# Two-layer metaformer with a mixture of experts: the taps of the second image's convolution moved from TensorE to VectorE, and its scatters paced

## The chip, the cores and the metric

The kernel runs on one core of one Trainium2 chip. The metric is the device time of one execution in microseconds; the lower the better. A core has TensorE (PE, matrix products; PEld is its weight load), VectorE (DVE), ScalarE (ACT), GpSimd (POOL) and SyncE (SP), which only issues transfers. Each has its own queue of instructions, and they meet through semaphores. Times of the kernel before are the median of three runs; the profile is of one execution of its own.

## The reference

The input is four images of 384 channels and 32 × 32 pixels, all in float32. Two layers follow, each a mixer and then a feed-forward part, with a residual sum around each:

```
x = x + attention(LN_c(x))           # layer 0, 8 heads, relative positions
t = t + kron_ffn(LN_t(t))
x = x + conv(LN_c(x))                # layer 1: 7x7 + 5x3 + 3x5 + 7x1*1x7 + 5x1*1x5, per channel
t = t + moe(LN_t(t))                 # 4 experts, best 2 of each token
```

The five convolutions of layer 1 act on each channel alone, so their sum is one 7 × 7 convolution with 49 taps per channel (folded beforehand in the kernel). The mixture of experts sends each of 4 × 1024 tokens to the two experts with the highest gate (384 → 1536 → 384 with a gelu between) and adds the two results, weighted by the gates.

## The kernel before

Channels lie on the 128 partitions in three chunks (`k`), tokens along the free axis. The attention runs first (to about 1540 us of the profiled execution) and the change doesn't touch it. Everything below is in `rest_phase`.

**Per image.** `front` (project L977, net L999 to L1030) loads an image and its attention result, projects, runs the first feed-forward network in two halves of 512 tokens, and `normalise` (L1051) prepares the layer norm of the convolution. `image` (L1065) writes the normalised image into the padded tile `img`, of which there is one. `convolve` (L1079) runs the 49 taps on VectorE: one `scalar_tensor_tensor` (L1089) per tap and part, where a part is some rows of one chunk; 32 rows are 1024 columns. `taps_by_matmul` (L1125) does taps on TensorE instead, with diagonal 64 × 64 weights, two taps to a pair (`tap_ps`, L1137), a sum over both halves (`taps_ps`, L1148) and an addition by VectorE (L1151). The diagonals lie in the second expert weight buffer `wts[1]`, so this buffer is not free for experts until the last such matmul. `gates` (L1184) computes the gate logits (`gate_ps`, L661) and picks two experts per token; `scatter` (L1223) works out each token's place and writes its rows out by 16 indirect transfers that GpSimd issues one by one (`write`, L1205). `dispatch` is `gates` and `scatter` together. These are Python generators: each `yield` is a step, and most give a pair of estimated costs (VectorE, TensorE) in us.

**Experts.** The scattered rows form 67 blocks of 128 rows, in four groups of 13, 16, 16 and 22 (`COUNTS`). Group g can begin when image g's scatters are done: its first gathers (`xg`, L1250) wait for all of them. A block is 12 steps of 6 + 2 matmuls (`e_ps` L1301, `y_ps` L1279), with gelu on ScalarE between (L1304) and the output's bias on VectorE (`yo`, L1282). Weights come in halves by indirect transfers on GpSimd's queue (L1269), three ahead; where the expert stays the same as two blocks before, the transfer moves nothing.

**Order.** The tile framework orders instructions per engine by program order unless an instruction is free to move up; `pin` and `keep_in_program_order` hold an instruction where it was written. In `convolve` the taps of image 0 alone are pinned. In the later images a tiny `pause` memset per step (L1097) is kept in order. `first` runs image 0's convolution with TensorE's taps and image 1's front between its steps. Then `dispatch(0)` is issued with image 1's TensorE taps and image 2's front dealt among its steps. The rest is one long generator, `todo = others()`: the convolution of images 1 to 3 with the front of the next image and the dispatch of the one before between the taps. The blocks call `more` 12 times each; it adds 0.05 to `clock[0]` (VectorE's account) and 1.36 to `clock[1]` (TensorE's) and takes steps from `todo` while the first is below the second, each step adding its costs. So the costs and the clock's starting values fix in which block a step is issued. At the end of a group, steps are taken until the next image's scatters are issued.

**Split of the taps before.** Image 0: VectorE chunk 0 and 24 rows of chunk 1, TensorE chunk 2 and 8 rows of chunk 1. Image 1: TensorE 16 rows of chunk 2, VectorE the rest. Images 2 and 3: VectorE alone.

Of the kernel before, what the change touches and what calls it, by code (L numbers as in the profile page):

```python
# [19 lines left out]
B, C, IMG = 4, 384, 32  # L20
N = IMG * IMG
NT = B * N
KC = C // P
# [77 lines left out]
def result(steps):  # L101

    while True:
        try:
            next(steps)
        except StopIteration as end:
            return end.value
# [786 lines left out]
def rest_phase(tc, cst, x, ao_d, ins, xs_d, y_d, x2_d, out):  # L894
# [9 lines left out]
    with ExitStack() as es:  # L904
# [11 lines left out]
        def pin(ins_):  # L916
            return tc.keep_in_program_order(ins_)
# [161 lines left out]
        def convolve(b, xb, parts):  # L1079


            with tc.issue_after(marks[b]) if b in marks else nullcontext():
                for k in range(KC):
                    nc.vector.tensor_scalar_add(xb[:, k, :], xb[:, k, :], cbias[:, k : k + 1])
            acc = xb.rearrange("p k (y x) -> p k y x", x=IMG)
            for dy in range(7):
                for dx in range(7):
                    for k, y0, y1 in parts:
                        ins_ = nc.vector.scalar_tensor_tensor(  # L1089
                            acc[:, k, y0:y1], img[:, k, dy + y0 : dy + y1, dx : dx + IMG],  # L1090
                            w7[:, k, dy, dx : dx + 1], acc[:, k, y0:y1], ALU.mult, ALU.add,
                        )
                        if not b:
                            pin(ins_)

                    if b:
                        tc.keep_in_program_order(nc.vector.memset(pause, 0.0))  # L1097
                    yield sum(0.12 + 0.0337 * (y1 - y0) for _, y0, y1 in parts) + 0.06, 0.0
            if b + 1 < B:
                nc.sync.dma_start(x2_d[:, b * N : (b + 1) * N].rearrange("(k p) n -> p k n", p=P), xb)  # L1100


        wts = [[wp.tile([P, WROW], F32, name=f"w{i}{fh}") for fh in range(2)] for i in range(2)]

        def preload(w, keep=lambda ins_: ins_, which=range(2)):
            for fh in which:
                keep(nc.sync.dma_start(w[fh], ins["w12"][fh * P : (fh + 1) * P, :]))
# [17 lines left out]
        def taps_by_matmul(xb, made, parts):  # L1125


            half, diag = made
            for k, y0, ny in parts:
                n = ny * IMG  # L1130
                sums = [ps_y.tile([P, TOK], F32, tag="y", name="tap_ps", bufs=2) for _ in range(2)]
                for t0 in range(0, 49, 2):
                    for t in range(t0, min(t0 + 2, 49)):
                        dy, dx = divmod(t, 7)
                        for h in range(2):
                            lo = 64 * h
                            nc.tensor.matmul(  # L1137
                                sums[h][64 * (t % 2) : 64 * (t % 2) + 64, :n].rearrange("p (y x) -> p y x", x=IMG),
                                diag[k][lo : lo + 64, t, :],
                                img[lo : lo + 64, k, dy + y0 : dy + y0 + ny, dx : dx + IMG],  # L1140
                                start=(t < 2), stop=(t > 46),
                            )
                    yield
                po = ps_y.tile([P, TOK], F32, tag="t", name="taps_ps")
                for h in range(2):
                    e = hid.tile([P, TOK], F32, tag="hs", name="taps", bufs=HS)
                    nc.scalar.copy(e[:, :n], sums[h][:, :n])
                    nc.tensor.matmul(po[64 * h : 64 * h + 64, :n], half, e[:, :n], start=True, stop=True)  # L1148
                yield
                acc = xb[:, k, y0 * IMG : y0 * IMG + n]  # L1150
                nc.vector.tensor_tensor(acc, acc, po[:, :n], ALU.add)  # L1151
                yield
# [31 lines left out]
        def gates(b):  # L1184

            xb, im = xbs[b], images[b]
            rows = [new_row() for _ in range(nj)]
            logits = ps_m.tile([P, TOK], F32, tag="m", name="logits_ps")
            yield from gate_logits(nc, (ps_m, hid), ident, gw, xb, logits)
            mean, rstd = yield from token_stats(nc, stp, ident, xb, cst["eps5"], rows, 2)  # L1190
            shift = small.tile([P, nj, 1], F32, tag="g_shift", name="g_shift")
            nc.vector.scalar_tensor_tensor(shift, mean, -1.0, rstd, ALU.mult, ALU.mult)
            yield from gate_weights(nc, small, logits, gb, rstd, im["mask"], im["top"])
            for j, row in enumerate(rows):
                nc.scalar.activation(row, row, AF.Identity, bias=shift[:, j, :], scale=rstd[:, j, :])
                im["rows"].append(row)
                if b and j % 2:
                    yield 0.0, 0.0
            yield 0.0, 0.0

        def new_row():
            return hid.tile([P, C], F32, tag="rows", name="rows", bufs=16)
# [171 lines left out]
        xbs, marks = {}, {}  # L1374

        def enter(b):
            xbs[b] = xp_.tile([P, KC, N], F32, tag="xb", name="xb")
            yield from front(b, xbs[b])

        def dispatch(b, pause=0.0):  # L1380
            yield from gates(b)
            yield from scatter(b, pause)

        def ahead(b, halves):
            if b < B:
                yield from enter(b)
                yield from normalise(xbs[b], halves)

        def first(halves, later):


            half, own = IMG // 2, 24
            taps = taps_by_matmul(xbs[0], made, [(2, 0, half), (2, half, half), (1, own, IMG - own)])
            yield from image(halves)
            for i, _ in enumerate(convolve(0, xbs[0], [(0, 0, IMG), (1, 0, own)])):
                for _ in range(1 + i % 4 // 2 + (i % 7 == 0)):
                    next(taps, None)
                if i % 7 < 5:
                    next(later, None)
                if i == 48:  # L1400
                    for steps in (taps, later):
                        for _ in steps:
                            pass
                yield
            preload(wts[1], which=(1,))

        def others():

            half, later = IMG // 2, iter(())
            for b in range(1, B):
                if b > 2:
                    yield from image(halves[b])
                side, later = later, ahead(b + 1, halves[b + 1]) if b > 1 else iter(())
                parts = [(k, 0, IMG) for k in range(KC - 1)] + [(KC - 1, half if b == 1 else 0, IMG)]
                for t, cost in enumerate(convolve(b, xbs[b], parts)):
                    for start, steps in ((2, side), (12, later)):
                        more = next(steps, None) if t >= start else None  # L1420
                        if more:
                            cost = cost[0] + more[0], cost[1] + more[1]
                    yield cost
                yield from side
                yield from later
                later = dispatch(b, 0.0 if b + 1 < B else 2.6)
                if b == 1:
                    yield next(later)
                    yield from image(halves[2])
                    yield from later  # L1430
            yield 6.0, 0.0
            yield from later
# [6 lines left out]
        halves = [[] for _ in range(B + 1)]  # L1439
# [11 lines left out]
        for _ in combined:  # L1451
            pass
        center(nc, ps_m, "m", one, gw)
        todo = others()
        made = diagonals((2, 1))
        for _ in first(halves[0], ahead(1, halves[1])):
            pass
        taps, later = taps_by_matmul(xbs[1], made, [(2, 0, IMG // 2)]), ahead(2, halves[2])
        for i, _ in enumerate(dispatch(0)):
            if i == 0:  # L1460
                result(image(halves[1]))
            for steps in (taps, taps, taps, later, later, later) if i > 5 else ():
                next(steps, None)
        for steps in (taps, later):
            result(steps)
        preload(wts[1], which=(0,))
        clock = [0.0, 25.0]

        def spend(steps):
            cost = next(steps, None)  # L1470
# [125 lines left out]
```

## Time and profile before

| | |
|---|---|
| median of 3 runs | 3109.57 us (3109.04 to 3110.0) |
| the profiled execution | 3105.85 us, span 3104.1 us |
| mean TensorE clock granted in it | 0.975 |
| attention and what precedes it | 0 to 1540 us |
| image 0's convolution, to its gates | 1590 to 1738 us |
| image 0's dispatch, to the first expert matmul | 1738 to 1854.5 us |
| expert blocks | 1854.5 to 3072 us |

The page gives the busy time of each engine, the span in 40 slices, the chain of work that ended last (followed back from the last instruction to what released it), and groups of instructions with the idle time before them and what ended it. A group name such as `xb L1089` is the tile written and the source line. In a table of windows the columns are PE, PEld, DVE, ACT and POOL busy time with the number of instructions, the mean granted clock of TensorE, the share of the transfer engines in use, and GB/s. A line of a waits table reads: engine and what it wanted to run, what it waited for, us in total, times, the longest. In a chain, a line is start, length and what ran.

### The profile page before, as it was taken

Reading aid. Unit: us, or ns where it says so; the run is one execution under the profiler, and the core shown is the slowest. Engines: PE = TensorE matmul, PEld = TensorE weight load, DVE = VectorE, ACT = ScalarE, POOL = GpSimd, SP = SyncE. Lnnn points to the kernel's source line nnn. Section 1 sums busy time; section 2 is a strip of 40 time slices with the busy share of each in tenths; the row PEclk is TensorE's granted clock in tenths of the full one; section 3 lists DMA queues with packets and bytes.
Section 4 is the critical chain, followed back from the end, with each engine's and each line's share of the span. In section 5 each row is a group of like instructions: output and inputs, shape, how many; then the busy total and the mean of one; then the engine's idle time right before and its main releaser. Section 6 shows DMA issues by size and latency. Waiting matters only on the chain.

```text
span 3104.1 us, 63791 instructions
## 1 busy us (share of the span) xinstructions
PE 2943.5 (95%) x25591; PEld 2026.7 (65%) x25591; DVE 1936.6 (62%) x3576; ACT 1375.3 (44%) x2835; POOL 1188.2 (38%) x1132
## 2 busy tenths in 40 slices
PE   8997999999999999999899789989999999999996
PEld 4544776767777777777533337765677777778775
DVE  2226777878787877787578899589999610001101
ACT  1105667666666666667312133423342423323332
POOL 3224737474747473737300142241126231214422
PEclk9998999999999999999999889999999999999998
DMA  3796565656565656564400324640445054475852
GB/s 125 261 318 207 133 199 130 207 130 207 132 206 134 203 134 193 134 203 120 176 21 1 117 74 151 249 156 16 168 153 199 29 186 169 149 288 198 307 193 73
DMA packets 262793, 500.56 MB, mean 161 GB/s; under 512 B 134737, under 2 KB 186833, under 8 KB 254817
## 3 DMA queue, kind: packets, MB, share of 16 engines
q1 hardware_dynamic: 169168, 247.12, 25.9%
q0 software_dynamic: 43424, 227.84, 19.9%
q10 hardware_dynamic: 49904, 21.53, 3.6%
q8 instruction: 201, 3.29, 0.5%
q14 instruction: 96, 0.78, 0.1%
HBM read 543.58 MB, written 152.37 MB: 224 GB/s over the span
## 4 chain that ended last, share of the span: by engine, by line
PE 76%; DVE 9%; issue 6%; DMA 4%; POOL 3%; ACT 2%; SPq 0%; POOLq 0%; ACTq 0%; DVEq 0%
PE e_ps L1301 16%; PE y_ps L1279 16%; PE t_ps L410 7%; PE sc_ps L227 7%; PE av_ps L227 7%; PE tabq_ps L227 5%; DVE xb L1089 4%; PE a_ps L420 3%; PE qk_ps L175 2%; PE tap_ps L1137 2%; PE proj_ps L977 2%; DMA s<-sd 2%; PE tv_ps L227 2%; POOL bias L353 1%; PE tabk_ps L227 1%
## 5 line engine op out<-in xcount | busy, mean ns | idle before, releaser
L1301 PEld LDWEIGHTS e_ps<-xT,w 128*128 128x128 f32 x4824 | 655.4, 192 | 224.6 <-DMA w<-in_w,row 12.1
L353 POOL TENSOR_TENSOR bias<-b,s 128x416 f32<-128x416 f32 (+24 forms) x656 | 660.2, 1044 | 179.0 <-DMA s<-sd 160.7
L1301 PE MATMUL e_ps<-xT,w 128*128 128x128 f32 x4824 | 670.4, 276 | 20.0 <-DMA w<-in_w,row 11.4
L1279 PE MATMUL y_ps<-w,eh 128*128 128x384 f32 x1608 | 652.6, 490 | 8.2 <-ACT eh L1304 8.2
L1089 DVE SCALAR_TENSOR_TENSOR xb<-img,pack,xb 128x1024 f32<-128x1024 f32 (+2 forms) x539 | 616.6, 1203 | 0.0
L1304 ACT ACTIVATE eh<-e_ps,w 128x128 f32<-128x128 f32 x804 | 294.4, 368 | 716.2 <-PE e_ps L1301 709.1
L1269 POOL DMA_INDIRECT w<-in_w,row x134 | 168.4, 1257 | 737.9 <-PE y_ps L1279 311.1
L402 DVE TENSOR_REDUCE extra<-arow 128x32 f32<-128x32 f32 (+24 forms) x768 | 381.0, 555 | 10.4 <-ACT arow L391 6.3
L381 DVE CUSTOM_DVE_ANT_0 arow<-sc_ps,bias 128x1024 f32<-128x1024 f32 x256 | 312.9, 1222 | 105.3 <-POOL bias L353 54.8
L410 PEld LDWEIGHTS t_ps<-ident,arow 128*128 128x128 f32 x2048 | 222.0, 142 | 176.1 <-ACT aT L411 100.6
L391 ACT ACTIVATE arow<-arow,nm 128x1024 f32<-128x1024 f32 x256 | 302.7, 1183 | 68.1 <-DVE nm L381 68.1
L1282 DVE TENSOR_TENSOR yo<-y_ps,w 128x384 f32<-128x384 f32 x67 | 37.2, 555 | 462.8 <-PE y_ps L1279 462.8
L411 ACT COPY aT<-t_ps 128x512 f32<-128x512 f32 x512 | 279.1, 604 | 96.2 <-PE t_ps L410 95.8
L410 PE MATMUL t_ps<-ident,arow 128*128 128x128 f32 x2048 | 283.9, 282 | 16.6 <-ACT arow L391 16.6
L227 PE MATMUL sc_ps<-kk,qs 48*32 48x512 f32 x4096 | 280.1, 610 | 7.2 <-DVE nm L381 6.2
L1279 PEld LDWEIGHTS y_ps<-w,eh 128*128 128x128 f32 x1608 | 247.5, 193 | 18.0 <-ACT eh L1304 10.0
L227 PEld LDWEIGHTS av_ps<-aT,vb 128*64 128x64 f32 x4096 | 222.3, 137 | 51.3 <-ACT aT L411 42.1
L227 PE MATMUL av_ps<-aT,vb 128*64 128x128 f32 x4096 | 237.7, 274 | 0.0
L318 DVE STREAM_TRANSPOSE b<-tabk_ps 128x480 f32<-128x480 f32 x256 | 218.3, 980 | 23.7 <-PE tabk_ps L227 22.4
L227 PE MATMUL tabk_ps<-tab,kq 48*128 48x480 f32 x512 | 223.1, 583 | 5.4 <-DVE b L318 5.4
L227 PE MATMUL tabq_ps<-tab,kq 48*128 48x480 f32 x512 | 220.2, 579 | 2.1 <-ACT aT L411 1.5
L1205 POOL DMA_INDIRECT xs_d<-rows,pos x64 | 92.3, 1442 | 263.6 <-DVE b_prod L860 239.5
(211 smaller groups left out, 3261.2 us busy)
## 6 DMA issues: line engine op xcount, KB each, us to landing
sd<-st SPq DMA_DIRECT2D x128, 480.0 KB, 2.5
s<-sd SPq DMA_DIRECT2D x256, 240.0 KB, 3.8
xs_d<-zero POOLq DMA_DIRECT2D x8, 3072.0 KB, 12.7
tvw<-in_tv SPq DMA_DIRECT2D x120, 192.0 KB, 4.2
y_d<-yo SPq DMA_DIRECT2D x67, 192.0 KB, 1.9
qk_d<-qk_sb POOLq DMA_DIRECT2D x48, 256.0 KB, 5.2
qs<-qk_d SPq DMA_DIRECT2D x256, 48.0 KB, 3.0
kq<-qk_d ACTq DMA_DIRECT2D x56, 192.0 KB, 3.9
```

The lines of the kernel that those rows point to most:

```text
L227: ins = nc.tensor.matmul(*args, **kw)
L318: turn = nc.vector.transpose(b2.rearrange("p e y x -> p x (e y)")[:, i + j], ps[:, j, : SPAN * IMG])
L353: nc.gpsimd.tensor_tensor(bias[:, y0:y1, :], bass.AP(b2.tensor, b2.offset + (e * IMG + y0) * IMG, [list(b2.ap[0]), [(step * IMG + 1) * IMG ...
L381: nc.vector.tensor_tensor_reduce(s["flat"], ps.rearrange("p h n -> p (h n)"), s["bias"].rearrange("p y x -> p (y x)"), -SCALE, BIG, ALU.ad ...
L391: nc.scalar.activation(s["flat"], s["flat"], AF.Exp, bias=s["nm"], scale=-1.0, accum_out=dn[:, y % YT : y % YT + 1])
L402: pin(nc.vector.tensor_reduce(ex[:, i, :], a[:, p0:p1, :].rearrange("p y x -> p x y"), AX.X, ALU.add))
L410: pin(nc.tensor.transpose(pt[:, j, :], s["flat"][:, k0 : k0 + P], ident))
L411: pin(nc.scalar.copy(aT[:, 4 * g : 4 * g + 4, s["y"] % YB, :], pt))
L1089: ins_ = nc.vector.scalar_tensor_tensor(acc[:, k, y0:y1], img[:, k, dy + y0 : dy + y1, dx : dx + IMG], w7[:, k, dy, dx : dx + 1], acc[:, k ...
L1279: nc.tensor.matmul(py, hs, w[:, o : o + C], start=(ff == 0), stop=(ff == NF - 1))
L1301: nc.tensor.matmul(ph, w[:, o : o + P], xT[k][:, c, :], start=(c == 0), stop=(c == KC - 1))
L1304: nc.scalar.activation(hs, ph, AF.Gelu, bias=w[:, o : o + 1])
```

## The change

1. Image 1's taps are pinned as image 0's are (`b <= 1`).
2. The cost that a step of taps announces is 0.16 + 0.035 per row and part in place of 0.12 + 0.0337 (for three whole chunks 3.90 in place of 3.66).
3. The steps of `gates` over the token rows announce 1.0 in place of 0.
4. Image 0: VectorE takes 52 rows (32 + 20), TensorE 12 rows of chunk 1 with its chunk 2, and an extra TensorE step comes every fifth tap in place of every seventh.
5. `preload` loads both halves of expert weights into `wts[1]` right after image 0's convolution, in place of one half there and one after `dispatch(0)`.
6. Image 1 is convolved by VectorE alone. While `dispatch(0)` and image 2's front are issued, from step 11 on one or two of three calls take one step of `todo` as well, 12 in all.
7. The clock starts at (0, −8) in place of (0, 25), and the steps between the scatter pairs announce 2.6 for image 1 (was 0) and 3 (as before), 0 for image 2 (as before).

```diff
@@ convolve
-                        if not b:
+                        if b <= 1:
                             pin(ins_)
...
-                    yield sum(0.12 + 0.0337 * (y1 - y0) for _, y0, y1 in parts) + 0.06, 0.0
+                    yield sum(0.16 + 0.035 * (y1 - y0) for _, y0, y1 in parts) + 0.06, 0.0
@@ gates
                 if b and j % 2:
-                    yield 0.0, 0.0
+                    yield 1.0, 0.0
@@ first
-            half, own = IMG // 2, 24
+            half, own = IMG // 2, 20
...
-                for _ in range(1 + i % 4 // 2 + (i % 7 == 0)):
+                for _ in range(1 + i % 4 // 2 + (i % 5 == 0)):
                     next(taps, None)
...
-            preload(wts[1], which=(1,))
+            preload(wts[1])
@@ others
-            half, later = IMG // 2, iter(())
+            later = iter(())
...
-                parts = [(k, 0, IMG) for k in range(KC - 1)] + [(KC - 1, half if b == 1 else 0, IMG)]
-                for t, cost in enumerate(convolve(b, xbs[b], parts)):
+                for t, cost in enumerate(convolve(b, xbs[b], [(k, 0, IMG) for k in range(KC)])):
...
-                later = dispatch(b, 0.0 if b + 1 < B else 2.6)
+                later = dispatch(b, 0.0 if b == 2 else 2.6)
@@ main
-        taps, later = taps_by_matmul(xbs[1], made, [(2, 0, IMG // 2)]), ahead(2, halves[2])
+        later = ahead(2, halves[2])
         for i, _ in enumerate(dispatch(0)):
             if i == 0:
                 result(image(halves[1]))
-            for steps in (taps, taps, taps, later, later, later) if i > 5 else ():
-                next(steps, None)
-        for steps in (taps, later):
-            result(steps)
-        preload(wts[1], which=(0,))
-        clock = [0.0, 25.0]
+            for j in range(3 if i > 5 else 0):
+                next(later, None)
+                if i > 10 and (i + j) % 2:
+                    next(todo)
+        result(later)
+        clock = [0.0, -8.0]
```

## The prediction

> **What bounds the kernel now.** I read the page's totals, its 40 slices, then the chain of waits and the table of windows for the stretch that the diff touches (1590 to 2475 us).
>
> ```profile
> PE 2943.5 (95%) x25591; PEld 2026.7 (65%) x25591; DVE 1936.6 (62%) x3576; ACT 1375.3 (44%) x2835; POOL 1188.2 (38%) x1132
> PE 76%; DVE 9%; issue 6%; DMA 4%; POOL 3%; ACT 2%; SPq 0%; POOLq 0%; ACTq 0%; DVEq 0%
> ```
>
> TensorE (PE) is the bound on average, so time is won only where it idles or does work that another engine can hide. The windows (TensorE, weight load, VectorE, ScalarE, GpSimd busy us, then clock) are image 0's convolution, its dispatch with image 2's front, and the expert blocks up to image 3's gates:
>
> ```profile
> 1590.00:1738.00 148.00, 125.47 (x788) 46.71 (x780) 134.01 (x163) 23.07 (x42) 0.00 (x0) 0.91 0.06 23
> 1738.00:1858.00 120.00, 109.00 (x483) 41.89 (x484) 103.92 (x214) 35.62 (x62) 41.99 (x25) 0.88 0.30 102
> 1858.00:2475.00 617.00, 589.51 (x3434) 438.86 (x3433) 538.05 (x920) 222.49 (x515) 176.31 (x123) 0.99 0.38 140
> ```
>
> The chain (start, length, what) and TensorE's waits name the limit of each:
>
> ```profile
> 1726.17 11.83 DVE xb L1089 x11
> 1738.14 5.29 PE gate_ps L661 x12
> ...
> 1749.38 5.42 PE tap_ps L1137 x42
> ...
> 1795.21 22.77 DVE xb L1089 x19
> ...
> 2038.80 10.89 DMA w<-in_w,row
> PE gate_ps L661 <- DVE xb L1089: 11.5, 1, 11.5
> PE e_ps L1301 <- DMA w<-in_w,row: 11.4, 1, 11.4
> ```
>
> In the first window VectorE's taps end last and TensorE stands 11.5 us. In the second, taps of image 1 on both engines lie on the path. In the third TensorE is full but for one late weight load, which this view of GpSimd's instructions explains:
>
> ```profile
> 2037.53 0.97 POOL L1205 DMA_INDIRECT xs_d<-rows,pos  x1 [0.30 <-issue]
> 2038.80 2.09 POOL L1269 DMA_INDIRECT w<-in_w,row  x1 [0.30 <-DVE xb L1089]
> 2041.20 2.08 POOL L1269 DMA_INDIRECT w<-in_w,row  x1 [0.31 <-issue]
> ```
>
> The loads stand behind image 1's 16 scatters (2010.2 to 2038.5).
>
> [...] the trace shows scatters of 0.97 us alternating with 2.02 us while taps run, whatever the cause.
>
> **Image 0's convolution.** VectorE takes 20 rows of chunk 1 in place of 24, 128 columns fewer per tap. Pitches in the trace: 1024 columns 1.196 us, 768 columns 0.929, 512 columns 0.66, so 128 cost 0.133; times 49 taps = −6.5 us. TensorE's third tap part grows from 256 to 384 columns: its 98 matmuls took 13.7 us at 256 and 25.7 at 512, so 19.7 now, +6.0. That is hidden in the 11.5 us idle before the gates (TensorE ends near 1723, VectorE at 1731.6); without that cover it would cost its 6. **−6.5**, between −4 (the last tap sums late) and −7.
>
> **Dispatch of image 0 with image 2's front.** From the gates at 1738.1 to the first expert matmul at 1854.5 is 116.4 us. Removed from TensorE: 196 tap matmuls (30.1 us) and their four sums (2.5 us). VectorE ran 51 taps of image 1 here (60.7 us); before, nothing but the scheduler's readiness placed them. Now they keep program order, and dealing them out puts seven steps of three taps (7 × 3 × 1.196 = 25.1 us, plus memsets of 0.06) ahead of that matmul. Demand falls to some 77 us on TensorE and 65 to 70 on VectorE, so neither fills the stretch. What is left is the front's chain. Stepped from the gates with its own durations: loads land at +9 to +11, positions done at +28, scatters to +55, first gather in at +62, first half of the network at +42 to +57, the second at +65 to +81, then layer statistics and the transposes: +93 to +96. **−22**. Cross-check: the chain carries 34.7 us of taps on VectorE and 16.6 on TensorE here; 51.3 gone and at most 25.1 back is −26 if all of it is on the path. Bounds: −32 if half the new taps are hidden, −10 if the network runs at half clock twice (18 us in place of 10 a half). The preload of both halves of expert 0's second buffer goes to SP earlier, ahead of the image-store and loads of the second front; 2.56 MB each, 10 us. It delays these loads by up to 10 us only if SP or the DMA engines hold them: the DMA share is 0.30 here and the window has 102 GB/s moved, so I take 1, inside the bounds above.
>
> **Expert blocks up to block 29.** A block is 12 × (0.67 + 0.65) plus its transposes, 16.1 us. Image 1's remaining 42 steps now run 4 to a block, and the raised cost per step (3.90 for 3.655) and the start of the clock at −8 for 25 fix how many. Gates of image 1 move from block 8 to 9.6, front 3 from 12.75 to 16.2, gates of image 2 from 18.75 to 22.75, of image 3 from 30.7 to 35.2.
> The pauses of 2.6 between image 1's scatters put them between weight loads (2, 4, 10) in place of 16 in one piece: the load for block 10 is no longer behind 28.3 us of scatters and the stall goes, **−11.4** (at worst 3 of it stay).
> VectorE pays: image 1's 49 steps whole. By pitches it needs 163 us from the first expert matmul to the end of that convolution and TensorE arrives after 158; with the gates' tail I take a wait of **+6** (0 to 10). The 12 and 15.6 us that VectorE idled before at blocks 6 and 7 are what hides the rest; image 1's taps cost 1.2 us each without it.
> Image 2's 16 scatters, split 2, 4, 4, 6 between loads before, stand in one piece now, right ahead of the second load and the gather of block 29. They start when VectorE has finished block 26's output and the positions, 16 × 1.8 = 28.8 us; load 2.1, issue and landing 4 to 5, transposes 1.1: block 29 starts 39 to 40 us after that output, against 32.8 undisturbed (two blocks and the bias add). **+7** (0 to 15). Queued behind these scatters are that load and gather alone, and TensorE waits for both.
> From block 29 on the order is the same and the 675.9 us from there stay; combining starts at block 52 as before. VectorE idles only 5 us from 2063 to 2446 now and carries four blocks' delay of the same work: bound 0 to +5, taken as 0.
>
> **Sum**: −6.5 − 22 − 11.4 + 6 + 7 = −26.9. TensorE's three gaps at image 1's gates now (0.7 + 1.6 + 0.4 = 2.7 us) are inside that 6 and come off: −29.6. The profiled execution of 3105.85 us (span 3104.1, 1.75 outside it) becomes 3076.3. The runs' median is 3.7 above it, so 3109.57 − 29.6 = 3080.0.
>
> **Rivals.** (a) *No boundary waits*: VectorE reaches image 1's gates in time and image 2's scatters run at the 1.28 us pitch seen beside a quiet VectorE: 13 us less, 3067 to 3070. For: my pitch sums are 2 us apart from TensorE's arrival. Against: VectorE is saturated at image 2's positions.
> (b) *The dispatch stretch doesn't shrink*: dealt taps sit in front of the front's own steps on an in-order engine, TensorE idles and its clock falls, as the half clock in 1821.8 to 1842.3 shows it can. Then it gives 0 to 10 us in place of 22; with −6.5, and −1.1 from the expert blocks, 3092 to 3102, taken as 3098.
> (c) *Slower*: VectorE becomes the bound at block 29. It takes over 16 image rows × 49 taps (32.3 us) from TensorE, and the group's gather waits for all 16 scatters after its positions. Its work from the first expert matmul to these positions is 514 us by pitches against TensorE's 533 to that point; with a surplus of 7 us hidden, each further microsecond of lateness is one of time. From 35 us late on (two blocks) the whole gain is gone; at 45 late, 3120. Against it: calibrated on the kernel before, the pitches gave 425.7 us for 423.6 busy.
> (d) *The change doesn't do what it says*: image 1's taps are pinned late but the clock lets them run into the gates anyway; the stretch shrinks, the load stall stays: 3092, inside (b)'s range.
>
> **How the numbers follow.** Main case 0.45 (own range 3074 to 3089), (a) 0.17, (b) with (d) 0.24, (c) 0.10, and 0.04 for the two halves cancelling near no change. The range 3062 to 3101 holds the main case, (a) nearly whole and most of (b): 0.8. A difference of 0.2% (6.2 us) is about what a measurement can tell: faster below 3103.4 takes the main case, (a), and nearly all of (b) and (d), 0.85; within it 0.05; slower above 3115.8, 0.10.
>
> **What would show it.** Right: TensorE's gap before the gates falls from 11.5 to some 5 us; from gates to first expert matmul 93 to 97 us in place of 116; no tap_ps after image 0; no wait for w at block 10; image 1's scatters in several pieces; a wait of some 7 us for xg or w at block 29 behind 16 scatters in one piece; the stretch from block 29 to the end within 3 us of 675.9. Wrong: a gap of 20 us or more at block 29 or at image 1's gates, or a clock of 0.5 through image 2's network.

## The result and the profile after

| | before | after |
|---|---|---|
| median of 4 runs | 3109.78 us (3109.04 to 3110.61) | 3082.49 us (3078.6 to 3092.57) |
| profiled execution | 3105.85 us, span 3104.1 | 3092.57 us, span 3090.6 |

The ratio is 0.9917, 95% interval 0.9893 to 0.9941: 0.6 to 1.1% faster, and 2.5 us from the predicted 3080.0. But the profiled execution of the changed kernel is its slowest run, only 13.3 us below that of the kernel before. So I took a second profile of the same kernel (first experiment, on a chip where the kernel before takes 3101 us). Both are set against the prediction stretch by stretch; where a stretch begins and ends is read off single instructions of the trace. Of the 37.9 us by which the second profile's span is shorter, some 4 lie ahead of the first tap, where nothing was changed; they are not in the table:

| stretch | before | predicted | first profile | second profile |
|---|---|---|---|---|
| first tap of image 0 to its gates | 146.2 | −6.5 | −1.7 | −2.1 |
| gates to first expert matmul | 116.4 | −22 | −22.7 | −21.2 |
| from there to block 29 | 573.7 | −1.1 | −10.0 | −10.7 |
| block 29 to block 50 | 356.0 | 0 | +3.6 | −2.0 |
| block 50 to block 61 (combining) | 190.1 | 0 | +17.1 | +2.1 |
| block 61 to the end | 129.6 | 0 | +0.1 | 0 |

The page's totals and chain by engine, after:

```profile
PE 2929.9 (95%) x25391; PEld 2020.6 (65%) x25391; DVE 1956.6 (63%) x3575; ACT 1370.8 (44%) x2833; POOL 1170.7 (38%) x1132
PE 67%; DVE 13%; issue 11%; POOL 4%; DMA 3%; ACT 2%; another core or an unknown queue 0%; SPq 0%; POOLq 0%; DVEq 0%; ACTq 0%
```

TensorE is busy 13.6 us less and VectorE 20 us more. The windows after (same columns as those of before: TensorE, weight load, VectorE, ScalarE, GpSimd, clock) of the first three stretches and of the combining:

```profile
1590.00:1736.70 146.70, 131.22 (x790) 46.10 (x791) 128.11 (x164) 23.35 (x43) 0.00 (x0) 0.95 0.11 41
1736.70:1830.40 93.70, 82.51 (x268) 32.34 (x269) 67.04 (x191) 32.88 (x57) 26.22 (x25) 0.81 0.31 104
1830.40:2394.10 563.70, 546.23 (x3185) 404.77 (x3184) 543.30 (x822) 201.29 (x472) 162.07 (x114) 0.99 0.41 151
2753.70:2960.90 207.20, 194.38 (x1167) 153.66 (x1166) 31.57 (x58) 64.59 (x167) 80.67 (x82) 0.98 0.58 206
```

The second line is the predicted shrinkage: 82.5 us of TensorE and 67 of VectorE in 93.7 us, so neither is full and the front's chain sets the length. These are the shares of that chain by line, from the gates to the first expert matmul, the kernel before first (the view cuts its own line off at the end):

```profile
by line: DVE xb L1089 29.9%; PE tap_ps L1137 12.2%; PE f_ps L1012 8.6%; PE proj_ps L977 7.0%; PE row_ps L87 5.9%; PE o_ps L1016 5.6%; PE gate_ps L661 4.6%; PE u_ps L999 3.2%; DVE s_st L89 2.6%; PE ffn_ps L1029 2.5%; PE taps_ps L1148 2.1%; D
```

```profile
by line: PE f_ps L1012 19.7%; PE o_ps L1016 15.7%; DVE xb L1089 7.1%; PE proj_ps L977 5.7%; PE row_ps L87 5.3%; DVE s_st L89 5.1%; PE gate_ps L661 4.9%; PE ffn_ps L1029 4.6%; DVE xb L980 4.2%; issue 3.4%; PE all_ps L117 3.3%; DVE xb L1030 2
```

Taps of both engines, 51.3 us of this chain before, are 6.7 us after. The two groups of matmuls of image 2's network (`f_ps` and `o_ps`) are 16.5 us of it before and 33.1 after: the taps no longer stand in front of them, and they run in part at half clock (0.50 from 1775 to 1787 us and from 1802 to 1815; the mean in this stretch is 0.81).

In the third window, VectorE is busy 543 of 564 us and TensorE still 546. TensorE's waits before and after, from the first expert matmul to block 29 (us in total, times, longest), the kernel before first:

```profile
...
PE e_ps L1301 <- DVE xb L1030: 3.4, 2, 2.0
PE y_ps L1279 <- ACT eh L1304: 3.1, 4, 1.6
PE xT_ps L1263 <- DMA xg<-xs_d,slot: 2.8, 2, 1.9
...
```

```profile
PE e_ps L1301 <- DVE xb L1030: 5.0, 2, 2.7
PE y_ps L1279 <- ACT eh L1304: 4.8, 4, 1.7
PE xT_ps L1263 <- DMA xg<-xs_d,slot: 4.0, 1, 4.0
...
PE e_ps L1301 <- DMA w<-in_w,row: 0.6, 1, 0.6
...
```

The 11.4 us for a weight load are gone, but for 0.6. The wait of 4.0 for `xg` is at block 29. GpSimd's queue just ahead of it, after:

```profile
2385.34 0.97 POOL L1205 DMA_INDIRECT xs_d<-rows,pos  x1 [0.30 <-issue]
2386.62 2.10 POOL L1269 DMA_INDIRECT w<-in_w,row  x1 [0.30 <-issue]
2389.03 1.03 POOL L1250 DMA_INDIRECT xg<-xs_d,slot  x1 [0.30 <-DVE xb L1089]
```

and the chain of waits there:

```profile
2389.03 3.48 DMA xg<-xs_d,slot
2392.50 0.14 issue
2392.64 0.89 PE xT_ps L1263 x3
```

The last of image 2's 16 scatters, then the load, then the gather: the predicted order, and the predicted wait at 4.0 us in place of 7.

### The profile page after: what moved, and what is told of

It reads as the page before. It is cut to its first block, busy times and chain, and to the rows that moved or that the text cites. A ratio compares the mean times of both kernels' runs of the same rounds, so it can differ in the third digit from the quotient of the medians.

```text
span 3090.6 us, 63376 instructions
## 1 busy us (share of the span) xinstructions
PE 2929.9 (95%) x25391; PEld 2020.6 (65%) x25391; DVE 1956.6 (63%) x3575; ACT 1370.8 (44%) x2833; POOL 1170.7 (38%) x1132
## 4 chain that ended last, share of the span: by engine, by line
PE 67%; DVE 13%; issue 11%; POOL 4%; DMA 3%; ACT 2%; another core or an unknown queue 0%; SPq 0%; POOLq 0%; DVEq 0%; ACTq 0%
PE e_ps L1301 12%; PE y_ps L1279 12%; DVE xb L1089 8%; PE t_ps L410 7%; PE av_ps L227 7%; PE sc_ps L227 7%; PE tabq_ps L227 5%; PE a_ps L420 3%; PE tv_ps L227 2%; PE proj_ps L977 2%; PE tabk_ps L227 1%; PE tap_ps L1137 1%; DVE extra L402 1%; PE f_ps L1012 1%; PE o_ps L1016 1%
## 5 line engine op out<-in xcount | busy, mean ns | idle before, releaser
L1089 DVE SCALAR_TENSOR_TENSOR xb<-img,pack,xb 128x1024 f32<-128x1024 f32 (+1 forms) x539 | 634.7, 1241 | 0.0
L410 PE MATMUL t_ps<-ident,arow 128*128 128x128 f32 x2048 | 283.2, 282 | 17.1 <-ACT arow L391 17.0
L1279 PEld LDWEIGHTS y_ps<-w,eh 128*128 128x128 f32 x1608 | 248.3, 193 | 31.9 <-ACT eh L1304 19.4
L322 ACT COPY st<-tabq_ps 128x480 f32<-128x480 f32 x256 | 142.3, 560 | 71.0 <-PE tabk_ps L227 45.0
```

The source lines that it names most:

```text
L410: pin(nc.tensor.transpose(pt[:, j, :], s["flat"][:, k0 : k0 + P], ident))
L1089: ins_ = nc.vector.scalar_tensor_tensor(acc[:, k, y0:y1], img[:, k, dy + y0 : dy + y1, dx : dx + IMG], w7[:, k, dy, dx : dx + 1], acc[:, k ...
L1279: nc.tensor.matmul(py, hs, w[:, o : o + C], start=(ff == 0), stop=(ff == NF - 1))
```

## The experiments

The kernel before took 3101, 3099, 3116 and 3114 us on the chips of the four sets of runs, so each run is given by its ratio to the kernel before on its own chip, and its stretches by the profile.

**The changed kernel again.**

> The changed kernel once more, unchanged, for a second profile. Theory: the 17 us that its first profile lost in blocks 50 to 61 (207.2 us for 190.2 before) are late gathers or instruction supply that differ from run to run, so this profile shows another figure for those blocks (190 to 205) and the same as the first elsewhere within 1 us (gates to first expert matmul 93.7, first expert matmul to block 29 563.7). Rival: the changed order of ScalarE's row weighing among the blocks costs it every time, then 207 again. Time 3078 to 3092.

0.989 (0.9874 to 0.9907); the profiled execution took 3068.15 us. Gates to first expert matmul 95.1, then 563.1 to block 29, and blocks 50 to 61 192.2 us in place of 207.2. So 15 of the 17 us there are of that execution, or of its chip, and not of the change. This window is of blocks 50 to 61 in the second profile,

```profile
2744.20:2936.40 192.20, 188.35 (x1165) 149.42 (x1164) 31.74 (x58) 65.55 (x168) 80.44 (x82) 1.00 0.62 222
```

with TensorE idle 4 us in place of 13 and its matmuls at full clock. In the first profile ScalarE stood still twice where the combining weighs its first rows. Its instructions there, with the idle time before each in brackets:

```profile
2785.88 0.37 ACT L1304 ACTIVATE eh<-e_ps,w 128x128 f32<-128x128 f32 x1 [3.23 <-PE e_ps L1301]
2790.14 0.62 ACT L1304 ACTIVATE eh<-e_ps,w 128x128 f32<-128x128 f32 x2 [3.89 <-remote]
2790.65 0.61 ACT L1352 ACTIVATE rows<-rows,gate 128x384 f32<-128x384 f32 x1
```

(`remote` is a releaser that the profile can't name.) The gathers of these rows had been issued from 2775.8 on, and late gathers come to mind. But the gelus that start late (`eh`) run ahead of the first row's weighing (`rows`), so late rows don't explain these two waits, and what does stays open. The same blocks took 190 to 192 us in the eight profiles of the first two sets of runs below and 197 to 203 in the four of the last two sets (both parts together, the two without dealing at image 2's old cost, the front sooner): they differ by chip or execution more than by kernel. The five profiles with the long combining have one more thing in common: they hold no landing time of any transfer, so their records have gaps, and what ended a wait may be missing in them. The kernel before has no profile on the chips where they were long, so whether it loses as much there stays open.

**Edit 4 alone.**

```diff
-            half, own = IMG // 2, 24
+            half, own = IMG // 2, 20
-                for _ in range(1 + i % 4 // 2 + (i % 7 == 0)):
+                for _ in range(1 + i % 4 // 2 + (i % 5 == 0)):
```

> The kernel before with edit 4 alone: 52 rows of image 0 on VectorE and an extra tap step of TensorE every fifth tap. As predicted: the convolution of image 0 from its first tap to the gates takes 146.2 - 6.5 = 139.7 us. By the new profile: 144.5, because VectorE waits longer for image 1's front, which TensorE reaches later. Everything after it moves along, so -6.5 or -1.5 us in the end; from the gates to the first expert matmul 116 us as before in both.

0.9987 (0.9978 to 0.9996); first tap to gates 143.4 us, −2.8. The taps did get shorter (a pair of them starts 1.991 us after the one before in place of 2.126, so 6.6 in 49). What ate the rest is seen in VectorE's longest waits from the first tap to the gates. Before and after:

```profile
DVE xb L1030 <- PE ffn_ps L1029: 5.3, 2, 3.9
```

```profile
DVE xb L1030 <- PE ffn_ps L1029: 9.7, 2, 5.9
```

VectorE's order holds two steps of image 1's network among the taps, and TensorE reaches that network later in relation to them. VectorE then stands in front of taps that it could do. This wait repeats from one execution to the next: it is 5.3 us in all four profiles with the order of before and 9.7 in all seven with edit 4 and nothing else changed here. The length of the stretch varies more, from 142.5 to 144.5 us among the six profiles of the changed kernel and its variants that leave this stretch as it is.

**The same rows, without TensorE's larger part.** VectorE's second part ends at row 20 while TensorE keeps rows 24 to 31, so four rows of chunk 1 are left out.

```diff
-            for i, _ in enumerate(convolve(0, xbs[0], [(0, 0, IMG), (1, 0, own)])):
+            for i, _ in enumerate(convolve(0, xbs[0], [(0, 0, IMG), (1, 0, own - 4)])):
```

> The kernel before with VectorE taking 52 rows of image 0 while TensorE keeps its 8 rows of chunk 1 and its pace: four rows of chunk 1 are convolved by nobody, so part of the computation is left out. It asks whether VectorE's 6.5 us were eaten by TensorE's larger tap part. Theory (TensorE's 128 extra columns per tap delay image 1's front, for which VectorE then waits in its order): first tap to gates 139.5 to 140.5 us. Rival (VectorE waits for the front anyway, since it now comes to it sooner): 143 as with edit 4 alone.

141.5 us in its one execution, between the two: −4.7 of the 6.5. The wait for the network's output was 6.9 us. By these waits, TensorE's added columns and pace cost 2.8 us (9.7 less 6.9) that I had called hidden, and 1.6 more (6.9 less 5.3) come because VectorE arrives sooner. The lengths say about the same, 2 us each, but that is no more than they vary.

**Pacing image 1's scatters alone.**

```diff
-                later = dispatch(b, 0.0 if b + 1 < B else 2.6)
+                later = dispatch(b, 0.0 if b == 2 else 2.6)
```

> The kernel before with a pause of 2.6 between image 1's scatter pairs, nothing else. Theory: the weight load of block 10 or 11 is no longer behind the 16 scatters, so TensorE's wait of 11.4 us for it goes and blocks 0 to 14 take 264 us in place of 275. The rest of the order moves a little. Rival: the load is late for another reason, or the scatters then come late for group 1; then 275 stays, or block 13 waits. Time 3098 or 3110.

0.9935 (0.9919 to 0.9952), −20 us, more than I expected. First expert matmul to block 29 takes 556.3 us (before 573.7) and to block 50 another 353.1 (356.0). TensorE's waits in the first of these begin

```profile
PE e_ps L1301 <- DVE xb L1030: 3.8, 2, 2.0
PE y_ps L1279 <- ACT eh L1304: 3.0, 4, 1.6
...
```

with neither w nor xg among them: 11.4 and 2.8 us gone, 14.2 of the 17.4 up to block 29. Blocks 0 to 14 fell by more (241 for 275) and blocks 14 to 29 rose, since image 3's front moved across the line. This is one line of code and worth 20 us.

**Image 1's taps on VectorE alone, nothing else.**

```diff
-                parts = [(k, 0, IMG) for k in range(KC - 1)] + [(KC - 1, half if b == 1 else 0, IMG)]
+                parts = [(k, 0, IMG) for k in range(KC - 1)] + [(KC - 1, 0, IMG)]
-        taps, later = taps_by_matmul(xbs[1], made, [(2, 0, IMG // 2)]), ahead(2, halves[2])
+        taps, later = iter(()), ahead(2, halves[2])
```

> The kernel before with image 1's taps wholly on VectorE and none on TensorE, nothing dealt out and the old clock. Theory: the stretch from the gates to the first expert matmul falls from 116 to 95 to 100 us, since taps on TensorE and the VectorE taps let up by them made it long; blocks 0 to 29 take longer than in the kernel before by some of the 32 us that VectorE takes over, with image 1's 16 scatters still in one piece: 575 to 590 us. Rival: the dealing among the front's steps is what shortens the stretch, then it stays above 105.

0.9899 (0.9882 to 0.9916), −31. The window from its gates to its first expert matmul:

```profile
1741.24:1831.05 89.81, 82.76 (x267) 32.32 (x268) 74.16 (x193) 34.16 (x58) 33.68 (x25) 0.80 0.32 108
```

That is below both expectations, and without any dealing: it is taking the taps from TensorE that shortens this stretch. VectorE's own taps in it, which nothing but readiness places, fell with it from 50 to 28, so how much of the 26.6 us is due to each engine's taps isn't separated. To block 29 it took 565.4 us, less than before in spite of 32 us more on VectorE and the scatters in one piece (the expectation of 575 to 590 missed): the convolution ends later, so the last scatter is issued 208 us after the first expert matmul in place of 183 and meets other loads, and the wait for a weight load is 3.3.

**Both of these.**

> The kernel before with two parts of the change alone: image 1 convolved by VectorE alone, and the pause of 2.6 between its scatter pairs. Alone they gave 31 us and 20 us. Theory: these two hold nearly all of the change's gain, and overlap, since VectorE's longer work on image 1 already moves its scatters: gates to first expert matmul 90, first expert matmul to block 29 555 to 562, time 3060 to 3068. Rival: without the new costs and clock VectorE's lateness brings back a wait of 5 us or more at image 1's gates or the weight load: 565 to 573 us, time 3068 to 3076.

0.9902 (0.9883 to 0.9921). 90.4 and 559.2 us, as the theory has it, but blocks 29 to 50 took 368.0 in place of 356 and the combining 197, so that the whole, 3085.2 us, misses the expected 3060 to 3068 and is by its ratio no better than the second alone. 8.6 us of the former are TensorE's waits for nothing recorded, at matmuls that need gelus; I leave them open.

**No dealing.**

```diff
-                if i > 10 and (i + j) % 2:
+                if False:
-        clock = [0.0, -8.0]
+        clock = [0.0, 39.4]
```

> The changed kernel with the 12 steps of image 1's taps not dealt out among image 2's front but left to the first block, with the clock raised by their cost so that what follows keeps its place. Theory: the dealt taps run in VectorE's idle time of that stretch, so the stretch itself shrinks by no more than 3 us without them (91 to 95), and the taps come back as a delay later in the blocks of up to 20 us. Rival: the seven steps stood on the front's chain (25 us of taps), then the stretch falls to 75 to 85.

0.9877 (0.9854 to 0.9899), not slower than the changed kernel. The stretch took 90.1 us and blocks 0 to 29 564.9 (563.1 with dealing). TensorE waited 9.2 us for gathers, once at block 10 and once at block 29, and other waits fell:

```profile
PE xT_ps L1263 <- DMA xg<-xs_d,slot: 4.4, 1, 4.4
```

```profile
PE xT_ps L1263 <- DMA xg<-xs_d,slot: 4.8, 1, 4.8
```

With dealing there is no wait at block 10 and one of 4.0 at block 29. Neither the rival's 75 to 85 nor the delay of up to 20 us came. Dealing steps out is worth nothing that I can measure.

**The old cost of a step, for all images.**

```diff
-                    yield sum(0.16 + 0.035 * (y1 - y0) for _, y0, y1 in parts) + 0.06, 0.0
+                    yield sum(0.12 + 0.0337 * (y1 - y0) for _, y0, y1 in parts) + 0.06, 0.0
```

> The changed kernel with edit 2 undone for all images (0.12 + 0.0337 per row), which issues image 1's gates some 9 us of account earlier, and image 2's scatters in four pieces of 4. Theory (VectorE decides when image 1's gates can run): TensorE waits longer at these gates, 5 to 10 us more than the 2.8 of the changed kernel, and the wait of 4 us at block 29 goes: first expert matmul to block 29 564 to 569 us. Rival (VectorE has slack there): the gates move up without a wait and it is 556 to 559, as with the old cost for image 2 alone or better.

0.992 (0.9903 to 0.9937), on a chip like that of the second profile (0.989). 566.7 us to block 29, within the theory's range. TensorE waits in that stretch, among others,

```profile
PE y_ps L1279 <- ACT eh L1304: 6.0, 5, 1.7
...
PE gate_ps L661 <- DVE xb L1089: 3.1, 1, 3.1
PE e_ps L1301 <- DMA w<-in_w,row: 2.8, 2, 2.2
...
```

A wait for VectorE's taps at gates now exists (in the changed kernel there is none), of 3.1 us and not the 5 to 10 expected, and that for `xg` is gone. VectorE does limit how early image 1's gates can stand, and the new cost sets them about where it arrives.

**The old cost for image 2 alone.** GpSimd's order then has its scatters as 2, 2 and 12.

```diff
-                    yield sum(0.16 + 0.035 * (y1 - y0) for _, y0, y1 in parts) + 0.06, 0.0
+                    yield sum((0.12 if b == 2 else 0.16) + (0.0337 if b == 2 else 0.035) * (y1 - y0) for _, y0, y1 in parts) + 0.06, 0.0
```

> The changed kernel with the old cost of a tap step (0.12 + 0.0337 per row) for image 2 alone, which issues its last steps some 12 us of account earlier: GpSimd's order then has image 2's 16 scatters as 2, 2 and 12 between loads in place of 16 in one piece. Theory: TensorE's wait at block 29 for the gather (4.0 + 0.6 us) goes, unless VectorE reaches the positions no earlier; then TensorE waits at image 2's gates instead and the sum to block 29 stays at 563.7. With the first: 559 us from the first expert matmul to block 29.

0.9864 (0.9847 to 0.988): 3060.67 us beside 3069.06 of the changed kernel on the same chip, with no overlap of their runs (3060.0 to 3061.0, 3066.1 to 3071.2). 558.4 us to block 29, and the wait there:

```profile
PE xT_ps L1263 <- DMA xg<-xs_d,slot: 0.7, 1, 0.7
```

The last of image 2's scatters is issued 549.3 us after the first expert matmul in place of 555.0; the gather and block 29 follow it as they did. Of the 8.4 us between the medians, the profiles put 4.7 up to block 29, as the theory has it, 2.8 in blocks 29 to 50 and 0.9 in the combining. This version beats both kernels.

**No dealing with that cost, and TensorE's pace.**

> The changed kernel with two parts altered: none of image 1's steps dealt out among image 2's front (clock raised by their cost), and the old cost of a step for image 2 alone, so that image 2's scatters stand as 2, 4 and 10 between loads. Theory: both savings add: gates to first expert matmul 90 us in place of 93.7 to 95, and TensorE's waits for gathers at block 29 (9.2 us without the dealing) go, so first expert matmul to block 29 is 556 to 559 us and the time 3050 to 3058 beside 3100 of the kernel before. Rival: the dealt taps come back as a wait at image 1's or 2's gates when block 29 no longer waits; then 563 and 3060 to 3064.

> As the run before, with TensorE's extra tap step for image 0 every seventh tap in place of every fifth, 52 rows kept. Theory: it is the columns and not the pace that hold VectorE up at image 1's front, so first tap to gates stays within 1.5 us of the other's 142.5 to 144.5. Rival: the denser tap steps stand ahead of the front on TensorE; then 140 to 141 and 2 to 4 us less in the end.

0.9861 (0.9837 to 0.9886) and 0.9859 (0.9835 to 0.9883): the same as the run with the cost alone. The savings did not add: 559.6 and 558.8 us to block 29. The wait at block 29 is gone in both, as the theory has it, but one of 4.6 (4.5) us for `xg` remains at block 10, where the run without dealing had 4.4 of its 9.2; the expectation had put all 9.2 at block 29. The pace changed nothing (144.5 and 144.6 us to the gates). But gates to first expert matmul was 83.9 in one and 91.0 in the other, with the same order of work there. The second half of image 2's network, the same 49 matmuls in both, makes 5.4 of these 7.1 us, and TensorE's clock differs in it (the third number from the end: 1.00 and 0.62):

```profile
1793.80:1806.30 12.50, 11.75 (x49) 3.32 (x50) 12.50 (x15) 6.65 (x13) 1.74 (x2) 1.00 0.09 25
```

```profile
1794.80:1812.70 17.90, 17.10 (x49) 4.50 (x50) 15.62 (x19) 6.77 (x13) 3.88 (x3) 0.62 0.08 22
```

**Image 1's front sooner.** With the old cost for image 2:

```diff
-                if i % 7 < 5:
-                    next(later, None)
+                next(later, None)
```

> The changed kernel with the old cost of a step for image 2 alone (as in the fourth run, 3060.7 beside 3101.0 of the kernel before, 0.986), and in image 0's convolution a step of image 1's front after every tap in place of five out of seven. Theory: edit 4's 6.5 us were lost because VectorE, in its order, waits for image 1's front on TensorE (9.7 us for the network's output alone); with the front issued sooner and ahead of tap steps these waits shrink, and first tap to gates goes from 144.5 to 139 to 142 us, the ratio to 0.985. Rival: the waits only move to other steps of the front, since the same work of TensorE stands between them; then 143.5 to 145.5 and the ratio stays 0.986.

0.9917 (0.9904 to 0.9931); first tap to gates 154.2 us, and both theory and rival are wrong. VectorE's waits and TensorE's before the gates:

```profile
DVE xb L1030 <- PE ffn_ps L1029: 14.0, 2, 7.7
DVE xb L1151 <- PE taps_ps L1148: 4.7, 1, 4.7
...
PE gate_ps L661 <- DVE xb L1089: 20.1, 1, 20.1
```

Issuing the front sooner puts VectorE's part of it sooner in VectorE's order as well, ahead of taps, while TensorE is no faster: the wait grows from 9.7 to 14.0, and a wait of 4.7 us for TensorE's tap sums comes to it. So the front was early rather than late for VectorE. To issue it later is what this points to, but that was not tried.

## Why the prediction was right, and where it was not

The sum was right (−29.6 against −27.3 in the medians; −31.9 on the chip of the second profile), but that it is so close is in part luck: image 0's convolution gave 4 to 5 us less than forecast and the blocks up to block 29 gave 9 to 10 more.

- **Image 0's convolution, −6.5: wrong in size.** It measured −1.7 and −2.1 in the two profiles and −2.8 alone. The step that failed is "that is hidden in the 11.5 us idle before the gates". I set TensorE's 6 us against idle time at the end of the stretch, though VectorE waits for TensorE in the middle of it (the table of waits of before had 5.3 us for `ffn_ps`). TensorE's gap before the gates fell only to 7.4 us, where I had said 5.
- **Dispatch and front, −22: right,** −21 to −23. Both sums of busy time were near (77 and 65 to 70 predicted, 82.5 and 67 measured), and the stepped chain gave 93 to 96 for 93.7 and 95.1. But what makes up the length is not what I had stepped. I let up to 25.1 us of dealt taps come back on the chain, and 6.7 came. I had the two halves of the network from +42 to +57 and from +65 to +81; in the first profile they run from +34 to +54 and from +62 to +81, sooner and longer, because part of both runs at half speed (a granted clock of 0.50), which I had only as a lower bound and, through the whole network, as a sign of being wrong. That the fewer taps and the longer network cancel is luck. The length is softer than I made it, too: 84 to 95 us over the variants without image 1's taps on TensorE, with the clock of TensorE in the network (1.00 or 0.62 in its second half) as one visible cause.
- **Weight load behind image 1's scatters, −11.4: right,** −10.8 by the waits.
- **VectorE at image 1's gates, +6: too high.** TensorE's waits there are 2.8 us (2.5 for gelus, 0.3 for rows), as much as before, none of it on the taps. The run with the old cost shows that the limit is real but that the gates stand about where VectorE arrives.
- **Image 2's scatters in one piece, +7: right in kind,** 4.0 measured. The order came out as forecast, image 1's scatters as 2, 4 and 10 and image 2's in one piece. I used a pitch of 1.8 us; the 16 took 24.9 us, 1.55 each, midway to the 1.28 of rival (a). I had left out that the pieces among loads cost the kernel before 2.8 us of waits for gathers too.
- **From block 29 on, 0: not so.** "The order is the same" was wrong, and at odds with the forecast that image 3's gates move from block 30.7 to 35.2, as they did; and ScalarE weighs the first combined rows two gelus later (behind 624 in place of 622). In the second profile it comes to 0 in sum, in the first to +20.8, most of which the same kernel's second profile doesn't show. Rival (c), lateness of VectorE at block 29, did not occur: 543 us busy in 564, and 4 us of wait.

The length of the network goes with TensorE's clock: in the kernel before, 24 matmuls on `f_ps` took a median of 0.640 us each from 1793.5 to 1804.3, at a clock of 1.00, and another 24 took 1.135 from 1823.0 to 1842.3, at 0.50. What sets the clock isn't shown. In the kernel before it fell to 0.50 while TensorE stood idle: at 1719.4, 2.0 us after the taps' end at 1717.4, and at 1821.8, 3.8 us into a gap of 5.0. It then stayed at 0.50 from 1823.0 to 1842.3, though TensorE was busy 17.8 of these 19.3 us. In the first profile of the changed kernel it fell at 1774.6 and 1801.9 amid matmuls, with no idle time longer than 1.2 and 2.2 us just before. So rival (b), in which idleness lowers the clock, has two of these four falls for it.

The long scatters go with VectorE's taps: image 2's, issued while taps ran, took 0.97 to 2.09 us each in the kernel before, and image 3's 16, issued after the last tap, 0.97 to 1.08. Why isn't shown.

## What to carry to other kernels

Idle time at the end of the stretch (11.5 us) didn't hide more work in its middle here (1.7 to 2.8 us came of 6.5): before work is called covered, look for waits of the other engine on this one inside the stretch. GpSimd issues its transfers one after the other here (scatters of 0.97 to 2.02 us with 0.30 between them in the profile after), so a long run of them (16 scatters, 24.9 us) is better cut between the loads that feed the bound engine: one line did that for 20 us. And two changes that remove the same wait don't add: pacing alone gave 556.3 us to block 29, image 1's taps on VectorE alone 565.4, both together 559.2.

## What was not expected of the hardware

The changed kernel took 3078.6 to 3092.6 us in its first four runs, and the kernel before had medians of 3099 to 3116 us in the sets of this study, with up to 14 us between runs of one set; the combining of rows, 11 blocks, took either 190 to 192 us or 197 to 207, and the same work ahead of the first expert matmul took 83.9 or 91.0 us, 5.4 us of the difference in one half of a short network that ran at a clock of 1.00 or 0.62.
